# Relational layers of a four-layer graph network: dense columns in four chunks of 448, tables stored by half block and loaded whole

## The chip, the core and the metric

The kernel runs on one core of a Trainium2 chip. The metric is the time of one execution on the device in microseconds (us). The kernel before was timed three times: 2260.39 us in the median, 2258.17 to 2264.78. Its profile was taken from one more execution, which took 2260.0 us with a profiled span of 2258.2 us.

## What is computed

The input is a graph of N = 3125 nodes with 128 features, and 100,000 edges. Each edge has a source, a destination and one of 8 types; the edges are sorted by destination. Four layers follow one another, each with a residual sum and a layer norm. The change concerns the fourth alone, two relational convolutions:

```python
def rgcn_layer(x, src, dst, etype, W, W_root, b, num_rels):
    h = jnp.einsum('ni,rio->rno', x, W)
    msg = h[etype, src]
    seg = dst * num_rels + etype
    sums = jax.ops.segment_sum(msg, seg, num_segments=N * num_rels)
    cnt = jax.ops.segment_sum(jnp.ones(msg.shape[0], x.dtype), seg, num_segments=N * num_rels)
    mean = sums / jnp.maximum(cnt, 1.0)[:, None]
    agg = mean.reshape(N, num_rels, do).sum(axis=1)
    return agg + x @ W_root + b
...
h = jax.nn.relu(rgcn_layer(x, src, dst, edge_type, W1, root1, b1, 8))    # 128 -> 256
x = _layernorm(x + rgcn_layer(h, src, dst, edge_type, W2, root2, b2, 8)) # 256 -> 128
```

For each destination and each type, the features of its sources are averaged, and the averages go through that type's weights.

## The kernel before

**Stages.** Up to about 430 us the kernel builds, from the edge list, a matrix of edge counts between all nodes. From there to about 940 us the first three layers multiply by this matrix, five times. Beside these products a generator, `relations`, builds one table of counts for each type: `rel[r]` holds, for 14 of the 25 blocks of 128 destination nodes, how many edges of type r run from each of the 3200 (padded) sources. The entries are bytes; a block is stored as 128 rows (the source within its block) of 25 x 128 bytes (source block, destination). These 14 blocks are the dense columns. The other 11 blocks are the gathered ones: nothing is stored for them, and their edges are fetched one by one. At about 1014 us the two relational layers begin, layer 1 to about 1716 us, layer 2 to the end.

**Dense columns.** The 14 blocks are worked on in four chunks of 4, 3, 4 and 3 blocks, so 512, 384, 512 and 384 columns (the first four entries of `CH`, called `DENSE`). One call of `relation` takes one type and one chunk; it is called a pass here. There are 32 passes in each layer, numbered 0 to 63 over both. In layer 1 the chunk is the outer loop and the type the inner one, so passes 0 to 7 are chunk 0, passes 8 to 15 chunk 1, and so on. In layer 2 the type is outer and the chunk inner. A pass has five groups of five source blocks. For each group the sync queue (SP) loads a piece of the table into one of six buffers `m8` (L725); VectorE (DVE, L735, groups 0, 2 and 4) or ScalarE (ACT, L733, groups 1 and 3) casts the bytes to floats in one of three buffers `m`; and TensorE (PE, L738) runs ten matmuls, one with the high part and one with the low part of the features of each source block. VectorE then multiplies the pass's sum by the inverse counts, which the ACT queue has loaded (L853 in layer 1, L914 in layer 2, where L916 adds the result to the output).

**Gathered columns.** A second generator, `gathered`, handles these edges 128 at a time, 355 times in each layer: GpSimd (POOL, L772) fetches 128 rows of the features by an indirect DMA into one of twelve buffers `gx`, VectorE makes a one-hot matrix of destination and type (`oh`, L764), and three or six matmuls (L780) add the rows up. After each group of a pass the generator is moved on by 2.2 steps on average, beginning with a debt of 14 steps, so about 11 gathers belong to a pass and some 28 are left behind the last pass of a layer. When a chunk of gathered blocks is complete, its sums are scaled (`put1`, `put2`).

**Between the layers.** In layer 1, when all eight types of a chunk are done, `linear1` multiplies by the weights: transposes of the features (L812), 36 matmuls over the chunk's columns (L818, L820), relu (L821). Then, for each whole block, it makes the features that layer 2 needs for all 8 types (L828, eight matmuls a block) and stores them with `store3`, twice a block, into `ht_d` (L715, on the SP queue, from two buffers `t3`). `store3` also writes the input of layer 1, `xt_d`, in seven stores at the start of layer 1; every gather of layer 1 waits for all seven, every gather of layer 2 for all stores to `ht_d`. In layer 2, `fetch` reads one type's features back in five loads `back` (L865, also SP, two buffers), adds the pieces on VectorE (L868, L869) and splits them in two.

**Order.** Instructions of an engine run in the order of the built program; each waits for its operands. The order is set by a scheduler at build time, from the order in the source and its own estimates. The SP queue holds, in one order, the loads L725, the stores L715 and the loads L865: one that waits for a buffer holds up those behind it.

Of the kernel before, what the change touches and what calls it, by code (L numbers as in the profile page):

```python
# [21 lines left out]
P = 128  # L22
D = 128
N = 3125
NB = 25
NP = NB * P
R = 8
# [30 lines left out]
SL = 64  # L58
HL = 49 * 64
ND = 14  # L60
# [12 lines left out]
def listed(ctx: ExitStack, tc: tile.TileContext, p: dict, out: bass.AP, bad):  # L73


    nc = tc.nc
# [4 lines left out]
    ident = const.tile([P, P], F32, name="ident")  # L81
# [17 lines left out]
    dsf = dram.tile([E // 200, 200], F32, name="dsf")  # L99
    adj = dram.tile([NB, P, NP], BF, name="adj")  # L100
    adj_t = dram.tile([NB, P, NB, P], BF, name="adj_t")
    rel = [dram.tile([ND, P, NB, P], U8, name=f"rel{r}") for r in range(R)]
    inv_d = dram.tile([R * SB, 2 * P], F32, name="inv_d")

    inv_n = dram.tile([SB * 2 * P, R], F32, name="inv_n")
# [42 lines left out]
    with tc.tile_pool(name="f_bg", bufs=1) as bg, tc.tile_pool(  # L148
# [194 lines left out]
        def relations():  # L343
# [95 lines left out]
            for i, (b, u) in enumerate(units):  # L439
                lo, hq = nxt  # L440
                if i + 1 < len(units):
                    nxt = hots(*units[i + 1])
                if u == 0:
                    rb = bg.tile([P, R * NB, 64], U16, name="rb", bufs=2)
                for v in range(PU // 4):
                    pt = psum.tile([P, 4, 256], F32, name="bld", tag="bld", bufs=2)
                    for k in range(4):
                        j = v * 4 + k
                        nc.tensor.matmul(pt[:, k, : R * NB], lo[:, j // 2, :, j % 2], hq[:, j // 2, :, j % 2],  # L449
                                         start=True, stop=True)  # L450
                    j0 = u * PU + v * 4
                    o = rb[:, :, j0 : j0 + 4]
                    src = pt[:, :, : R * NB].rearrange("p j q -> p q j")
                    n += 1
                    if n % 5 < 4:
                        nc.scalar.copy(o, src)  # L456
                    else:
                        nc.vector.tensor_copy(o, src)  # L458
                    if v == 1:
                        yield  # L460
                if u == 64 // PU - 1:
                    for r in range(R):
# [214 lines left out]

    O1 = 256
    x3 = xa
    DENSE = [c for c in CH if c[0] < ND]  # L680
    with tc.tile_pool(name="f_rel", bufs=1) as rp, tc.tile_pool(
        name="f_psr", bufs=1, space=PSUM
    ) as psum:
# [2 lines left out]
        b1 = column("L3_gnn_b1", 2)  # L686
        b2 = column("L3_gnn_b2")

        def load_inv(r, m0, nb):
            t = rp.tile([P, 512], F32, name="inv", bufs=2)  # L690
            v = inv_d.rearrange("r c -> (r c)")[r * SB * 2 * P + m0 * P :]
            nc.scalar.dma_start(t[:, : nb * P], bcast(v, nb * P))
            return t[:, : nb * P]

        def pair():
            t = rp.tile([P, 2, NB, D], F32R, name="hilo", tag="big", bufs=2)
# [19 lines left out]

        ahead = [0.0]

        def relation(r, m0, nb, pieces, work, rate):

            acc = psum.tile([P, 512], F32, name="acc", tag="acc", bufs=2)
            w = nb * P
            for g in range(5):
                m8 = rp.tile([P, 4, 5, P], U8, name="m8", bufs=6)
                nc.sync.dma_start(  # L725
                    m8[:, :nb].rearrange("p b k d -> p b (k d)"),
                    rel[r][m0 : m0 + nb, :, 5 * g : 5 * g + 5].rearrange("b p k d -> p b (k d)"),
                )
                m = rp.tile([P, 5, 4 * P + 8], F32R, name="m", bufs=3)
                v = m[:, :, :w].rearrange("p k (b d) -> p k b d", d=P)  # L730
                src = m8[:, :nb].rearrange("p b k d -> p k b d")
                if g % 2:
                    nc.scalar.copy(v, src)  # L733
                else:
                    nc.vector.tensor_copy(v, src)  # L735
                for k in range(5):
                    for i, x in enumerate(pieces):
                        nc.tensor.matmul(  # L738
                            acc[:, :w], x[:, 5 * g + k, :],
                            m[:, k, :w],  # L740
                            start=(g == 0 and k == 0 and i == 0), stop=(g == 4 and k == 4 and i == 1),
                        )
# [4 lines left out]
            return acc[:, :w]  # L747

        def gathered(table, rows, put):

# [39 lines left out]
        with tc.tile_pool(name="f_z", bufs=1) as zp:  # L790
# [13 lines left out]
                store3(xt_d[m0 * P : (m0 + nb) * P].rearrange("(b p) c -> p b c", p=P),  # L804
                       x3[:, m0 : m0 + nb, :])

            def linear1(z, m0, nb):
                w = min(nb * P, HL - m0 * P)
                x3t = zp.tile([P, 512], F32, name="x3t", bufs=1)
                t = psum.tile([P, 512], F32, name="mi", tag="mi", bufs=2)  # L810
                for i in range(nb):
                    nc.tensor.transpose(t[:, cols(i, 1)], x3[:, m0 + i, :], ident)  # L812
                nc.scalar.copy(x3t[:, : nb * P], t[:, : nb * P])
                for a in range(2):
                    o = psum.tile([P, 512], F32, name="mi", tag="mi", bufs=2)
                    c = slice(a * P, (a + 1) * P)
                    for r in range(R):
                        nc.tensor.matmul(o[:, :w], w1[:, r, c], z[:, r, :w],  # L818
                                         start=(r == 0), stop=False)
                    nc.tensor.matmul(o[:, :w], root1[:, c], x3t[:, :w], start=False, stop=True)  # L820
                    nc.scalar.activation(hT[:, a, m0 * P : m0 * P + w], o[:, :w], AF.Relu,  # L821
                                         bias=b1[:, a : a + 1])

                for b in range(m0, m0 + nb):
                    for r in range(0, R, 4):
                        o = psum.tile([P, 512], F32, name="mi", tag="mi", bufs=2)
                        for a in range(2):
                            nc.tensor.matmul(o, hT[:, a, cols(b, 1)],  # L828
                                             wr[:, a, r : r + 4, :].rearrange("p r c -> p (r c)"),
                                             start=(a == 0), stop=(a == 1))  # L830
                        store3(ht_d.rearrange("(r n) c -> n r c", r=R)[b * P : (b + 1) * P, r : r + 4],
                               blocks(o))
# [3 lines left out]
            def put1(b, wn, acc, inv):  # L836
                m0, nb = [c for c in CH if c[0] <= b < c[0] + c[1]][0]
                if b == m0:
                    zg[0] = zp.tile([P, R, 512], F32, name="z", bufs=2)
                o = zg[0][:, :, (b - m0) * P : (b - m0) * P + wn].rearrange("p r n -> p n r")  # L840
                nc.vector.tensor_mul(o, acc.rearrange("p (n r) -> p n r", r=R),
                                     inv.rearrange("p (n r) -> p n r", r=R))
                if b == m0 + nb - 1:
                    linear1(zg[0], m0, nb)

            work = gathered(xt_d, gsrc[0], put1)
            ahead[0] = -14
            for m0, nb in DENSE:
                z = zp.tile([P, R, 512], F32, name="z", bufs=2)
                for r in range(R):  # L850
                    inv = load_inv(r, m0, nb)
                    acc = relation(r, m0, nb, xs, work, 2.2)
                    nc.vector.tensor_mul(z[:, r, : nb * P], acc, inv)  # L853
                linear1(z, m0, nb)
            for _ in work:
                pass

        with tc.tile_pool(name="f_hr", bufs=1) as hp:
# [47 lines left out]
            hr = fetch(0)  # L906
            for r in range(R):
                nxt = None
                for i, (m0, nb) in enumerate(DENSE):
                    inv = load_inv(r, m0, nb)  # L910
                    acc = relation(r, m0, nb, hr, work, 2.2)
                    s = hp.tile([P, 512], F32, name="s", bufs=2)
                    w = nb * P
                    nc.vector.tensor_mul(s[:, :w], acc, inv)  # L914
                    c = cols(m0, nb)
                    nc.vector.tensor_add(oT[:, c], oT[:, c], s[:, :w])  # L916
# [624 lines left out]
```

## Time and profile before

| what | time |
|---|---|
| three timed runs, median | 2260.39 us |
| the profiled execution | 2260.0 us |
| its span | 2258.2 us |
| TensorE busy in the span | 1955.4 us (87%) |
| VectorE busy | 1376.9 us (61%) |
| GpSimd busy | 954.5 us (42%) |
| first matmul of a dense pass | at 1014.6 us |
| first and last gather of layer 1 | at 1053.7 and 1662.4 us |
| first and last gather of layer 2 | at 1715.6 and 2242.2 us |

The profile gives the span in us from the first instruction. A row of a group has the line, the engine, the operation, the tile written and the tiles read, the shapes and the count; behind the first bar stand the group's busy time and the mean duration of one in ns, behind the second the engine's idle time before these instructions and what ended it. Digits are dropped from the names, so `m<-m` is the cast from `m8` to `m`, and `m<-rel` the load of `m8`. PEld is the load of TensorE's stationary operand. A row of a stretch has its bounds, its length, then busy time and count of PE, PEld, DVE, ACT and POOL, the granted clock of TensorE, the busy share of the 16 DMA engines and the GB/s they moved. A row of waits has who waited for whom: us in total, times, longest.

### The profile page before, as it was taken

What the parts mean: (1) busy time and instruction counts of PE and PEld (TensorE: products, weight loads), DVE (VectorE), ACT (ScalarE), POOL (GpSimd) and SP (SyncE); (2) the same over time, 40 slices, a digit from 0 to 9 for tenths busy, and PEclk for the clock granted to TensorE, in tenths of its full rate; (3) what the DMA queues carried; (4) which work ended last, traced back from release to release, by engine and by line L of the source; (5) the groups of instructions that cost most, each with busy time, mean ns of one, the idle gap of its engine ahead of it and who ended that gap; (6) DMA issues with size and microseconds to landing.
All of it is one profiled execution on the core that took longest, in us unless ns stands there. A gap on an engine that the chain in (4) does not pass through costs nothing. (4 is left out here: it accounts for less than half of the span.)

```text
span 2258.2 us, 32584 instructions
## 1 busy us (share of the span) xinstructions
PE 1955.4 (87%) x12551; PEld 1351.3 (60%) x12551; DVE 1376.9 (61%) x2385; ACT 791.5 (35%) x1027; POOL 954.5 (42%) x898
## 2 busy tenths in 40 slices
PE   1666669999999999957999999999878998899894
PEld 1444436666665555445668667758745776777772
DVE  4888889999996430045435345435337776666663
ACT  1666734545442110044223233233224333232230
POOL 3222121211210000002757547727723887777875
PEclk9777779999999999978999999999989999999996
DMA  3444476887888666427657467637637887788762
GB/s 93 176 189 166 178 193 211 287 284 257 272 277 269 180 193 177 120 60 222 173 140 212 139 185 213 187 117 207 172 99 219 241 238 221 201 229 228 199 172 77
DMA packets 384638, 433.10 MB, mean 192 GB/s; under 512 B 28731, under 2 KB 350301, under 8 KB 384472
## 3 DMA queue, kind: packets, MB, share of 16 engines
q1 hardware_dynamic: 314318, 278.95, 40.7%
q0 software_dynamic: 45920, 119.66, 18.2%
q10 hardware_dynamic: 24234, 32.31, 5.0%
q8 instruction: 100, 1.64, 0.3%
q14 instruction: 66, 0.54, 0.1%
HBM read 319.22 MB, written 111.58 MB: 191 GB/s over the span
## 5 line engine op out<-in xcount | busy, mean ns | idle before, releaser
L738 PE MATMUL acc<-m,hilo 128*128 128x384 f32 (+1 forms) x3200 | 758.5, 383 | 12.0 <-DVE m L735 6.6
L772 POOL DMA_INDIRECT gx<-xt_d,gsrc x355 | 393.6, 1109 | 573.2 <-DMA m<-rel 357.2
L738 PEld LDWEIGHTS acc<-m,hilo 128*128 128x128 f32 x3200 | 577.6, 193 | 80.3 <-issue 8.9
L539 PE MATMUL acc<-m,parts 128*128 128x512 bf16 (+1 forms) x2625 | 539.3, 357 | 15.7 <-issue 12.7
L772 POOL DMA_INDIRECT gx<-ht_d,gsrc x355 | 412.9, 1163 | 167.0 <-issue 56.4
L733 ACT CAST m<-m 128x1920 fp32r<-128x1920 uint8 (+1 forms) x128 | 264.2, 2064 | 540.1 <-PE acc L738 491.5
L735 DVE CAST m<-m 128x2560 fp32r<-128x2560 uint8 (+1 forms) x192 | 302.6, 1576 | 161.3 <-PE acc L738 92.5
L539 PEld LDWEIGHTS <-parts 128*128 128x128 bf16 x2625 | 255.3, 98 | 238.3 <-issue 17.9
L780 PE MATMUL ga<-oh,gx 128*128 128x192 bf16 (+1 forms) x2442 | 273.5, 246 | 98.8 <-DMA gx<-ht_d,gsrc 57.7
L780 PEld LDWEIGHTS <-gx 128*128 128x128 bf16 x2442 | 170.7, 99 | 206.9 <-DMA gx<-ht_d,gsrc 83.1
L456 ACT CAST rb<-bld 128x800 uint16<-128x800 f32 x179 | 143.9, 828 | 129.7 <-PE bld L449 121.4
L463 POOL DMA_DIRECT2D rel<-rb x112 | 64.3, 582 | 287.5 <-ACT rb L456 162.6
L764 DVE TENSOR_TENSOR oh<-iota,gkey 128x768 bf16<-128x768 bf16 (+1 forms) x188 | 99.5, 530 | 92.2 <-PE ga L780 89.2
L162 DVE TENSOR_TENSOR lo<-iota,kT 128x2048 bf16<-128x2048 bf16 x100 | 122.0, 1220 | 0.0
L712 DVE TENSOR_TENSOR e<-mi,t 128x512 f32<-128x512 f32 x50 | 34.3, 688 | 133.8 <-ACT t L711 133.8
L272 PE MATMUL bld<-hi,lo 128*128 128x50 bf16 x1600 | 74.4, 200 | 46.1 <-DVE hi L162 38.9
L449 PE MATMUL bld<-rhq,rlo 128*128 128x200 bf16 x896 | 107.6, 252 | 1.8 <-DVE rb L458 1.1
L272 PEld LDWEIGHTS <-lo 128*128 128x128 bf16 x1600 | 63.4, 107 | 70.6 <-DVE hi L162 26.3
L449 PEld LDWEIGHTS <-rlo 128*128 128x128 bf16 x896 | 82.4, 98 | 36.7 <-issue 9.0
L162 DVE TENSOR_TENSOR rhq<-iota,kT 128x3200 bf16<-128x3200 bf16 x56 | 102.2, 1824 | 0.0
L828 PE MATMUL mi<-wr,hT 128*128 128x512 f32 x200 | 93.9, 604 | 4.8 <-DVE e L712 4.7
L285 ACT ACTIVATE av<-mi 128x896 bf16<-128x896 bf16 (+1 forms) x100 | 82.8, 835 | 31.4 <-PE mi L284 30.1
(212 smaller groups left out, 1813.4 us busy)
## 6 DMA issues: line engine op xcount, KB each, us to landing
m<-rel SPq DMA_DIRECT2D x160, 320.0 KB, 4.1
rel<-rb POOLq DMA_DIRECT2D x112, 400.0 KB, 6.5
m<-adj SPq DMA_DIRECT2D x60, 640.0 KB, 7.3
m<-rel SPq DMA_DIRECT2D x160, 240.0 KB, 3.2
m<-adj_t SPq DMA_DIRECT2D x40, 640.0 KB, 4.1
m<-adj SPq DMA_DIRECT2D x45, 480.0 KB, 6.1
adj_t<-at SPq DMA_DIRECT2D x25, 800.0 KB
adj<-av SPq DMA_DIRECT2D x25, 800.0 KB, 3.3
```

Of the source, the lines that this page charges most:

```text
L162: nc.vector.tensor_tensor(o, (iota2 if of is None else of)[:, None, :width, :].to_broadcast([P, PU // 2, width, 2]), k[:, :, None, :].to_b ...
L272: nc.tensor.matmul(pt[:, j, : 2 * NB], lo[:, j // 2, :, j % 2], hi[:, j // 2, :, j % 2], start=True, stop=True)
L449: nc.tensor.matmul(pt[:, k, : R * NB], lo[:, j // 2, :, j % 2], hq[:, j // 2, :, j % 2], start=True, stop=True)
L456: nc.scalar.copy(o, src)
L539: nc.tensor.matmul(o, x[:, k, :], m(k - k0), start=(k == 0 and i == 0), stop=last and more is None)
L733: nc.scalar.copy(v, src)
L735: nc.vector.tensor_copy(v, src)
L738: nc.tensor.matmul(acc[:, :w], x[:, 5 * g + k, :], m[:, k, :w], start=(g == 0 and k == 0 and i == 0), stop=(g == 4 and k == 4 and i == 1),)
L764: nc.vector.tensor_tensor(oh[:, : nt // 2], iota2[:, None, : GW * R, :].to_broadcast([P, nt // 2, GW * R, 2]), gkey[:, g, t : t + nt].rear ...
L772: nc.gpsimd.indirect_dma_start(out=gx.rearrange("p i c -> p (i c)"), out_offset=None, in_=table[:], in_offset=bass.IndirectOffsetOnAxis(ap ...
L780: nc.tensor.matmul(acc[:, a:z], gx[:, i, :], oh[:, t % 4 // 2, a - c0 : z - c0, t % 2], start=(a // 512 not in seen), stop=(t == GT[g] - 1 ...
L828: nc.tensor.matmul(o, hT[:, a, cols(b, 1)], wr[:, a, r : r + 4, :].rearrange("p r c -> p (r c)"), start=(a == 0), stop=(a == 1))
```

## The change

The tables `rel[r]` are stored by half blocks of 64 destinations: 28 half blocks, each 128 rows of 25 x 64 bytes, 1600 bytes in one run where a row of a block was 3200. The staging tile `rb` in `relations` is ordered to match, and each of its 112 stores writes two half blocks.

The dense columns are cut into four chunks of 7 half blocks, 448 columns each. A pass loads its whole table, 1400 KB in 7 x 128 runs of 1600 bytes, with one DMA into one of two buffers `m8`, in place of five loads of 320 or 240 KB in runs of 640 bytes into six buffers. The casts have 5 x 7 x 64 elements, the matmuls 448 columns. `linear1` takes its first column and width, and the list of blocks that are whole by then: 3, 4, 3 and 4 of them where it was 4, 3, 4 and 3. A chunk that starts or ends in the middle of a block transposes that block too, so 16 transposes in the four dense chunks and not 14. `load_inv` loads 448 columns each time. The gathers are as before.

```diff
-    rel = [dram.tile([ND, P, NB, P], U8, name=f"rel{r}") for r in range(R)]
+    rel = [dram.tile([2 * ND, P, NB, 64], U8, name=f"rel{r}") for r in range(R)]
...
-                    rb = bg.tile([P, R * NB, 64], U16, name="rb", bufs=2)
+                    rb = bg.tile([P, 2, R * NB, 32], U16, name="rb", bufs=2)
...
-                    o = rb[:, :, j0 : j0 + 4]
+                    o = rb[:, j0 // 32, :, j0 % 32 : j0 % 32 + 4]
...
-                            rel[r][b].rearrange("p s d -> p (s d)").bitcast(U16),
-                            rb[:, r * NB : (r + 1) * NB, :].rearrange("p s j -> p (s j)"),
+                            rel[r][2 * b : 2 * b + 2].rearrange("h p s d -> p h (s d)").bitcast(U16),
+                            rb[:, :, r * NB : (r + 1) * NB, :].rearrange("p h s j -> p h (s j)"),
...
-    DENSE = [c for c in CH if c[0] < ND]
+    CW = 7 * 64
+    DENSE = [(7 * i, 7 * i // 2, (7 * i + 7) // 2 - 7 * i // 2) for i in range(2 * ND // 7)]
...
-        def relation(r, m0, nb, pieces, work, rate):
+        def relation(r, h0, pieces, work, rate):
             acc = psum.tile([P, 512], F32, name="acc", tag="acc", bufs=2)
-            w = nb * P
+            m8 = rp.tile([P, 7, NB, 64], U8, name="m8", bufs=2)
+            nc.sync.dma_start(m8.rearrange("p h k d -> p h (k d)"),
+                              rel[r][h0 : h0 + 7].rearrange("h p k d -> p h (k d)"))
             for g in range(5):
-                m8 = rp.tile([P, 4, 5, P], U8, name="m8", bufs=6)
-                nc.sync.dma_start(
-                    m8[:, :nb].rearrange("p b k d -> p b (k d)"),
-                    rel[r][m0 : m0 + nb, :, 5 * g : 5 * g + 5].rearrange("b p k d -> p b (k d)"),
-                )
-                m = rp.tile([P, 5, 4 * P + 8], F32R, name="m", bufs=3)
-                v = m[:, :, :w].rearrange("p k (b d) -> p k b d", d=P)
-                src = m8[:, :nb].rearrange("p b k d -> p k b d")
+                m = rp.tile([P, 5, CW + 8], F32R, name="m", bufs=3)
+                v = m[:, :, :CW].rearrange("p k (h d) -> p k h d", d=64)
+                src = m8[:, :, 5 * g : 5 * g + 5].rearrange("p h k d -> p k h d")
...
-            def linear1(z, m0, nb):
-                w = min(nb * P, HL - m0 * P)
+            def linear1(z, c0, w, whole):
+                b0 = c0 // P
...
-                for i in range(nb):
-                    nc.tensor.transpose(t[:, cols(i, 1)], x3[:, m0 + i, :], ident)
-                nc.scalar.copy(x3t[:, : nb * P], t[:, : nb * P])
+                for b in range(b0, -(-(c0 + w) // P)):
+                    nc.tensor.transpose(t[:, cols(b - b0, 1)], x3[:, b, :], ident)
+                nc.scalar.copy(x3t[:, :w], t[:, c0 - b0 * P : c0 - b0 * P + w])
...
-                for b in range(m0, m0 + nb):
+                for b in whole:
```

More of the change, by code (lines that the diff above doesn't have):

```diff
@@ L687, in listed, with load_inv @@
         b2 = column("L3_gnn_b2")
[L689 to L693, printed above, removed]
+        def load_inv(r, h0):
+            t = rp.tile([P, CW], F32, name="inv", bufs=2)
+            v = inv_d.rearrange("r c -> (r c)")[r * SB * 2 * P + h0 * 64 :]
+            nc.scalar.dma_start(t, bcast(v, CW))
+            return t
         def pair():
@@ L738, in relation @@
                         nc.tensor.matmul(
-                            acc[:, :w], x[:, 5 * g + k, :],
-                            m[:, k, :w],
+                            acc[:, :CW], x[:, 5 * g + k, :], m[:, k, :CW],
                             start=(g == 0 and k == 0 and i == 0), stop=(g == 4 and k == 4 and i == 1),
@@ L746, in relation @@
                     ahead[0] -= 1.0
-            return acc[:, :w]
+            return acc[:, :CW]
         def gathered(table, rows, put):
@@ L820, in linear1 @@
                     nc.tensor.matmul(o[:, :w], root1[:, c], x3t[:, :w], start=False, stop=True)
-                    nc.scalar.activation(hT[:, a, m0 * P : m0 * P + w], o[:, :w], AF.Relu,
+                    nc.scalar.activation(hT[:, a, c0 : c0 + w], o[:, :w], AF.Relu,
                                          bias=b1[:, a : a + 1])
-                for b in range(m0, m0 + nb):
+                for b in whole:
                     for r in range(0, R, 4):
@@ L843, in put1 @@
                 if b == m0 + nb - 1:
-                    linear1(zg[0], m0, nb)
+                    linear1(zg[0], m0 * P, min(nb * P, HL - m0 * P), range(m0, m0 + nb))
             work = gathered(xt_d, gsrc[0], put1)
             ahead[0] = -14
-            for m0, nb in DENSE:
+            for h0, m0, nb in DENSE:
                 z = zp.tile([P, R, 512], F32, name="z", bufs=2)
                 for r in range(R):
[L851 to L854, printed above, removed]
+                    inv = load_inv(r, h0)
+                    acc = relation(r, h0, xs, work, 2.2)
+                    nc.vector.tensor_mul(z[:, r, :CW], acc, inv)
+                linear1(z, h0 * 64, CW, range(m0, m0 + nb))
             for _ in work:
@@ L908, in listed @@
                 nxt = None
[L909 to L916, printed above, removed]
+                for i, (h0, m0, nb) in enumerate(DENSE):
+                    inv = load_inv(r, h0)
+                    acc = relation(r, h0, hr, work, 2.2)
+                    s = hp.tile([P, CW], F32, name="s", bufs=2)
+                    nc.vector.tensor_mul(s, acc, inv)
+                    c = slice(h0 * 64, h0 * 64 + CW)
+                    nc.vector.tensor_add(oT[:, c], oT[:, c], s)
                     if i == 0 and r + 1 < R:
```

## The prediction

> **What bounds the kernel now.** I read the groups of the page first, for what a pass costs, then stretches of single chunks, then GpSimd's waits, then the timeline where the gathers begin. The change touches the span from 1014 us on; before it, only the order in which the tables are stored. The groups:
>
> ```profile
> L738 PE MATMUL acc<-m,hilo 128*128 128x512 f32 x1600 | 424.8, 411 | 6.2 <-ACT m L733 3.6 <-ACT hilo L702 1.6 <-DVE m L735 0.8
> L738 PE MATMUL acc<-m,hilo 128*128 128x384 f32 x1600 | 333.7, 355 | 5.8 <-DVE m L735 5.8
> L735 DVE CAST m<-m 128x2560 fp32r<-128x2560 uint8 x96 | 170.6, 1778 | 83.7 <-PE acc L738 51.2 <-ACT m L733 16.5 <-issue 13.2
> L735 DVE CAST m<-m 128x1920 fp32r<-128x1920 uint8 x96 | 131.9, 1374 | 77.6 <-PE acc L738 41.3 <-issue 29.7 <-ACT m L733 6.6
> L818 PE MATMUL mi<-z,w 128*128 128x512 f32 x96 | 42.3, 593 | 0.6 <-DVE z L841 0.6
> L818 PE MATMUL mi<-z,w 128*128 128x384 f32 x96 | 32.0, 487 | 0.6 <-DVE z L841 0.6
> L828 PE MATMUL mi<-wr,hT 128*128 128x512 f32 x200 | 93.9, 604 | 4.8 <-DVE e L712 4.7
> ```
>
> Behind the bar stand busy time and the mean of one, which counts the overlap with its neighbours; busy time over count is the cost: 265.5 ns a matmul at 512 columns (424.8 / 1600), 208.6 at 384. Now the stretches: passes 2-7 (chunk 0), 9-13 (chunk 1), 17-22 (chunk 2), 25-30 (chunk 3), and layer 2 whole.
>
> ```profile
> 1044.60:1158.30 113.70, 98.75 (x546) 72.87 (x546) 49.95 (x48) 28.89 (x15) 82.04 (x75) 0.94 0.64 176
> 1200.00:1266.30 66.30, 60.62 (x441) 54.71 (x438) 32.73 (x37) 17.96 (x10) 52.02 (x47) 1.00 0.71 197
> 1358.50:1446.20 87.70, 87.70 (x526) 68.88 (x524) 47.29 (x44) 28.00 (x12) 69.81 (x59) 1.00 0.76 207
> 1528.00:1609.50 81.50, 73.27 (x518) 64.90 (x515) 42.01 (x48) 23.17 (x15) 64.43 (x57) 1.00 0.71 196
> 1716.00:2243.00 527.00, 462.82 (x2834) 376.04 (x2832) 347.37 (x467) 158.14 (x109) 412.33 (x355) 0.94 0.75 208
> ```
>
> TensorE is idle for 14.95, 5.68, 0 and 8.23 us in layer 1's four chunks (length less the first busy time) and for 64.2 us in layer 2. What paces it there is GpSimd; first its waits in layer 1, then in layer 2, then its tile in layer 2:
>
> ```profile
> POOL gx L772 <- PE ga L780: 132.5, 80, 22.2
> ```
>
> ```profile
> POOL gx L772 <- PE ga L780: 31.2, 80, 6.6
> ```
>
> ```profile
> L772 POOL DMA_INDIRECT gx<-ht_d,gsrc x355: 940/948/2772, 1715.6 to 2242.2; - x178
> ```
>
> In layer 1 GpSimd stands still for 132.5 us with its twelve buffers full, mostly while TensorE works on `linear1`. In layer 2 it waits 31.2 us in 80 pieces, of which one is 6.6. It issues 355 gathers in 526.6 us, 1.48 us each, beginning to end. Layer 2 is set by the gathers, layer 1 by TensorE with gaps where gathers come late. The beginning of the gathers:
>
> ```profile
> 1044.92 3.72 SPq L725 DMA_DIRECT2D m<-rel  x2
> 1048.88 0.36 SPq L715 DMA_DIRECT2D xt_d<-t  x1
> ...
> 1053.71 1.05 POOL L772 DMA_INDIRECT gx<-xt_d,gsrc  x1 [357.22 <-DMA m<-rel]
> ```
>
> The seventh `xt_d` store is issued at 1048.88 behind loads of `m8` and lands just ahead of 1053.71, when GpSimd starts. The `m<-rel` named as its releaser is only what came last by the profile.
>
> **Costs that cancel.** A 448-column matmul is taken half way: (265.5 + 208.6) / 2 = 237 ns, so 3200 of them cost 758.5 us as before. The DVE cast is (1778 + 1374) / 2 = 1576 ns, 192 x 1.576 = 302.6 us, unchanged; ACT's (2331 and 1796, so 2064) likewise. That a cast out of 64-byte pieces keeps its rate no row shows. The two rows give 0.63 ns an element and 0.16 us besides; nothing speaks for less, and were it two thirds more (1.05 ns, so 2.5 us), DVE would be busy 347 + 96 x 0.93 = 436 of 527 us in layer 2, still not the bound. I take no change. The 112 table stores keep their bytes in twice as many runs; between 430 and 940 us TensorE is busy 507.8 of 510 us and POOL, which issues them, 50.1. That idle time hides them; without it they would cost 0.58 us each, 65 us.
>
> **Costs that move.** In the timeline of single records matmuls start 233 ns apart at 512 columns and 176 at 384, so 204.5 at 448: 28.5 ns x 50 = 1.4 us less for each pass of chunks 0 and 2, and 1.4 more in chunks 1 and 3. In `linear1`, 36 matmuls are 0.441 us at 512 and 0.333 at 384, so 1.9 us either way; a whole block at L828 is 8 x 0.47 = 3.8 us. With 3, 4, 3, 4 whole blocks: -5.8 us for chunks 0 and 2, +5.8 for 1 and 3. The two extra transposes are within a microsecond.
>
> **The load.** One DMA of 1400 KB replaces five. Rows: 320 KB in 4.1 us, 240 in 3.2, a slope that gives 16 us at 1400 KB; 640 KB of `adj_t` in runs of 1280 bytes 4.1, 480 KB 3.6, a slope that gives 6.5.
>
> ```profile
> m<-rel SPq DMA_DIRECT2D x160, 320.0 KB, 4.1
> m<-adj_t SPq DMA_DIRECT2D x40, 640.0 KB, 4.1
> m<-rel SPq DMA_DIRECT2D x160, 240.0 KB, 3.2
> m<-adj_t SPq DMA_DIRECT2D x30, 480.0 KB, 3.6
> ```
>
> I take 6.5 (its runs of 1280 bytes are nearest to 1600). With two buffers the load for pass r+2 is issued when the last cast of pass r is done, about 2/5 into TensorE's work on r, and needed a cast ahead of r+2: 1.6 passes less a cast, 1.6 x 13.1 - 2 = 19 us in layer 1, 23 in layer 2 at 15.5 a pass. Both prices fit, so I cost the wait at 0. The cover in layer 2 is 64.2/32 = 2 us of idle TensorE per pass; later than that, each microsecond counts.
>
> Behind that load on SP wait the `xt_d` and `ht_d` stores and the `back` loads. By the order of the built programs, the last `xt_d` store used to have its data written on DVE behind a cast of pass 2 and now behind the first cast of pass 3, for which TensorE must have come to matmul 130 in place of 100, and it stands behind the whole load for pass 4. The later data is 30 x 204.5 ns = +6.1 us; the narrower 100 matmuls give back 2.9; the first whole load costs +1 (0 to 4) at the start; the load ahead costs 0 to 3.5. Together +4, bounds 0 to +13.
>
> The Trainium skill, "DMA: Bandwidth & Descriptors", section on queues, rings and completion order, says that an engine's descriptors are consumed in ring order. By it that store's bytes wait for all 1.4 MB ahead, which at its derated 368 GB/s is an estimate of 3.9 us, and my sum would be +6 and not +2; no run here has yet shown so long a load.
>
> **Sum, as the shift of each landmark of layer 1.** Chunk 0 is paced by gathers, so its narrower passes gain nothing and its end shifts by the later start: +4. `linear1` -5.8: -1.8. Pass 8 +1.4; passes 9-13 +7.1, of which 5.7 fills idle time; passes 14-15 +2.8: +3.8, and 1 us of gaps there fills too: +2.8. `linear1` +5.8: +8.6. Chunk 2 would gain 8 x 1.4 = 11.3, but its 13.1-us passes receive 13.1 / 1.42 = 9.2 gathers where 10.7 are due (1.42 us is GpSimd's pace in layer 1), and twelve full buffers cover only that many; I take -8, bounds -11.3 to -4.5: +0.6. `linear1` -5.8: -5.2. Chunk 3 +11.3 less its 8.2 idle: -2.1. The last `linear1` +5.8: +3.7; but in pass 31 TensorE stood 10.4 us for gathers (its timeline), which can take up what came before; I let it take 3.7 (bounds 0 to 10.4), so layer 1 ends at 0. The `ht_d` stores held behind a whole load delay the first gather of layer 2 by a third of its 6.5 us: +2 (bounds 0 to 6.5). In layer 2 the gathers set the pace and are not changed: 0 (bounds -8, with the 6.6-us wait gone and a little more, to +8, were each gather 1.5% slower in the bursts of the loads). Sum: 2260.0 + 2 = **2262 us**; the profiled execution is 0.4 below the median, so both bases give this.
>
> **Rivals.** (1) *Faster: balance pays.* The start shifts by 1 and not 4, chunk 2 gains its full 11.3, and of pass 31's waits another 5 are filled: 2262 - 3 - 3.3 - 5 = 2250. For it: 13.9 us of idle time in the two narrow chunks. Against: it is the gathers that are late there, and equal passes don't bring more of them. (2) *Slower: a late start.* The gathers begin at the upper bound, +13, and each stretch stays gather-paced: 2262 + 9 + 4 = 2275. For it: the 357 us in which GpSimd waits for that one chain. Against: the 132.5 us in which it later waits for buffers. (3) *Slower: whole loads are late.* In layer 2 a load stands on SP behind `back` loads, which in the timeline wait up to 14 us for their two buffers; with the 16-us price that makes 30 against a window of 23, so 7 us late twice at each of seven fetches, less 8 us of cover in a type's four passes: 7 x (14 - 8) = 42, 2304. It decides once delay and load together exceed 23 + 2 us. For it: five pieces spread over six buffers need no such window. Against: at 6.5 us, 20.5 fits. (4) The change doesn't do what it says, each long load breaking up into short transfers: then it costs 16 us, without a delay inside the window, and the time is 2262 again, so it has no chance of its own.
>
> **How the numbers follow.** A measurement of this kernel tells about 0.3%, 6.8 us, from no change. Forecast (2253 to 2267, no change) 0.38; rival 1 0.29; rival 2 0.20; rival 3 0.13. Faster 0.29, same 0.38, slower 0.33. Below 2246 lies a fifth of rival 1 (0.06), above 2284 rival 3 and a little of rival 2 (0.14), so the range is 2246 to 2284.
>
> **What would show it.** The first gather of layer 1 at about 1058; TensorE's idle time below 6 us in chunk 3 but some 3 in chunk 2; dense matmuls busy 758 us; DVE's cast at 1576 ns; the load landing in some 6.5 us with no idle time of casts put down to it; 355 gathers of layer 2 in 527 us. The forecast is wrong if layer 2 grows by more than 8 us (then a load or the gathers' bursts set it), or if the gathers of layer 1 start later than 1067.

## The result, and the profile after

The changed kernel takes 2270.39 us in the median of seven runs (2264.66 to 2275.25), the kernel before 2260.39; the ratio is 1.0046, with an interval of 1.0034 to 1.0057. It is slower, by 0.5%. The profiled execution took 2268.9 us with a span of 2267.1, 8.9 us more than before. First the groups of the page that answer to those of before:

```profile
L738 PE MATMUL acc<-m,hilo 128*128 128x448 f32 x3200 | 770.2, 387 | 9.4 <-DVE m L735 4.7
L771 POOL DMA_INDIRECT gx<-xt_d,gsrc x355 | 395.7, 1115 | 578.7 <-DMA inv<-inv_d 359.4
L771 POOL DMA_INDIRECT gx<-ht_d,gsrc x355 | 417.3, 1175 | 164.0 <-issue 62.7
L735 DVE CAST m<-m 128x2240 fp32r<-128x2240 uint8 x192 | 301.7, 1572 | 131.8 <-PE acc L738 121.2
```

The cast costs what the two old shapes give half way (1572 ns, 1576 forecast), so pieces of 64 bytes are no burden to it. The dense matmuls are busy 11.7 us longer than the 758.5 forecast. The whole load, in the page's list of DMA issues:

```profile
m<-rel SPq DMA_DIRECT2D x64, 1400.0 KB, 7.5
```

The 7.5 us are the median of the 6 loads, of 64, whose landing the trace gives.

The stretches of the changed kernel, with the same passes as before: 2-7, 9-13, 17-22, 25-30, and layer 2 (columns as before: bounds, length, then PE, PEld, DVE, ACT and POOL, granted clock, DMA share, GB/s). Each begins with the first dense matmul of its first pass; the first ends with pass 7.

```profile
1041.60:1160.40 118.80, 95.95 (x540) 76.23 (x539) 44.77 (x46) 24.96 (x15) 81.38 (x76) 0.87 0.53 162
1198.40:1271.60 73.20, 68.64 (x441) 58.61 (x439) 34.74 (x37) 20.64 (x10) 57.97 (x51) 0.98 0.64 201
1370.90:1456.50 85.60, 80.07 (x525) 68.69 (x523) 44.52 (x46) 25.98 (x14) 67.83 (x58) 1.00 0.65 204
1531.30:1616.90 85.60, 81.18 (x518) 69.85 (x515) 46.85 (x49) 26.88 (x16) 67.79 (x59) 0.98 0.67 209
1723.50:2252.40 528.90, 465.40 (x2835) 389.44 (x2833) 347.40 (x466) 158.76 (x109) 416.79 (x355) 0.93 0.67 207
```

The first stretch, passes 2 to 7, is longer: TensorE is idle for 22.85 us of it (14.95 before), and its length is 118.8 us against 112.5 from the first dense matmul of pass 2 to the end of the last of pass 7 before. Chunk 2, whose passes had no idle TensorE at 512 columns, now has 5.5 us of it (85.6 less 80.1), and passes 17 to 22 are only 2.1 us shorter. Layer 2 is as long as before (528.9 against 527.0). The DMA engines are busy 0.64 to 0.67 of the time in the last four, for about the GB/s that took 0.71 to 0.76: long runs cost them less. Nothing was waiting for that.

Where the 10 us are is seen best by four distances from the clearing of `hT` (a MEMSET that marks the end of the layers before) to the last gather of layer 1. They are differences of start times in the traces; two profiles of each kernel, and two kernels of the experiments, are set beside each other:

| kernel | `hT` to first dense matmul | to the issue of the seventh `xt_d` store | to the first gather | first to last gather | sum |
|---|---|---|---|---|---|
| before | 10.6 | 34.2 | 4.8 | 608.7 | 658.3 |
| before, again | 10.4 | 34.3 | 4.6 | 608.6 | 657.9 |
| 448 columns, loads in pieces | 9.4 | 37.7 | 3.8 | 607.7 | 658.6 |
| changed | 14.2 | 34.3 | 6.0 | 614.0 | 668.5 |
| changed, again | 13.9 | 34.4 | 6.1 | 614.2 | 668.7 |
| old columns, whole loads | 14.7 | 36.5 | 6.2 | 612.4 | 669.8 |

In this table all kernels with whole loads have the 10 us, and none of the others has. From there on (the way to layer 2, and layer 2) they differ by some 3 us (595.8 to 599.0), without order.

### The profile page after: what moved, and what is told of

It is laid out like the page before. It is cut to its first block, busy times and chain, and to the rows that moved or that the text cites. A ratio compares the mean times of both kernels' runs of the same rounds, so it can differ in the third digit from the quotient of the medians.

```text
span 2267.1 us, 32002 instructions
## 1 busy us (share of the span) xinstructions
PE 1958.9 (86%) x12521; PEld 1377.5 (61%) x12553; DVE 1375.8 (61%) x2385; ACT 792.7 (35%) x1027; POOL 980.9 (43%) x898
## 4 chain that ended last, share of the span: by engine, by line
PE 55%; DMA 20%; DVE 13%; issue 6%; ACT 3%; POOL 3%; ACTq 0%; DVEq 0%; POOLq 0%
PE acc L738 19%; PE acc L540 17%; DMA gx<-ht_d,gsrc 8%; DMA gx<-xt_d,gsrc 6%; PE ga L779 5%; PE mi L818 4%; PE mi L828 3%; PE bld L450 2%; DVE lo L163 2%; DMA g<-dsf,irow 2%; POOL gx L771 2%; DVE hi L163 2%; DVE rhq L163 1%; PE mi L556 1%; DMA back<-ht_d 1%
## 5 line engine op out<-in xcount | busy, mean ns | idle before, releaser
L738 PE MATMUL acc<-m,hilo 128*128 128x448 f32 x3200 | 770.2, 387 | 9.4 <-DVE m L735 4.7
L771 POOL DMA_INDIRECT gx<-xt_d,gsrc x355 | 395.7, 1115 | 578.7 <-DMA inv<-inv_d 359.4
L738 PEld LDWEIGHTS acc<-m,hilo 128*128 128x128 f32 x3200 | 601.7, 196 | 60.2 <-issue 10.3
L540 PE MATMUL acc<-m,parts 128*128 128x512 bf16 (+1 forms) x2593 | 533.3, 357 | 17.6 <-issue 12.7
L771 POOL DMA_INDIRECT gx<-ht_d,gsrc x355 | 417.3, 1175 | 164.0 <-issue 62.7
L733 ACT CAST m<-m 128x2240 fp32r<-128x2240 uint8 x128 | 264.2, 2064 | 565.3 <-PE acc L738 495.9
L735 DVE CAST m<-m 128x2240 fp32r<-128x2240 uint8 x192 | 301.7, 1572 | 131.8 <-PE acc L738 121.2
L464 POOL DMA_DIRECT2D rel<-rb x112 | 84.9, 761 | 268.3 <-ACT rb L457 152.8
L715 DVE TENSOR_TENSOR e<-mi,t 128x512 f32<-128x512 f32 x50 | 34.3, 687 | 134.8 <-ACT t L714 131.2
```

What stands on the lines that cost most here:

```text
L540: nc.tensor.matmul(o, x[:, k, :], m(k - k0), start=(k == 0 and i == 0), stop=last and more is None)
L738: nc.tensor.matmul(acc[:, :CW], x[:, 5 * g + k, :], m[:, k, :CW], start=(g == 0 and k == 0 and i == 0), stop=(g == 4 and k == 4 and i == 1),)
L771: nc.gpsimd.indirect_dma_start(out=gx.rearrange("p i c -> p (i c)"), out_offset=None, in_=table[:], in_offset=bass.IndirectOffsetOnAxis(ap ...
```

## The experiments

Twelve runs were made, of ten kernels. Theory W, the first one formed after the result, put the cost on the equal widths; rival L on the whole loads.

**First four, on a chip that decided little.** The old columns with one whole load a pass (the small tile `x3t` shares the buffers of `e3`, for room):

```diff
+            m8 = rp.tile([P, 4, NB, P], U8, name="m8", bufs=2)
+            nc.sync.dma_start(m8[:, :nb].rearrange("p b k d -> p b (k d)"),
+                              rel[r][m0 : m0 + nb].rearrange("b p k d -> p b (k d)"))
             for g in range(5):
-                m8 = rp.tile([P, 4, 5, P], U8, name="m8", bufs=6)
-                nc.sync.dma_start(
-                    m8[:, :nb].rearrange("p b k d -> p b (k d)"),
-                    rel[r][m0 : m0 + nb, :, 5 * g : 5 * g + 5].rearrange("b p k d -> p b (k d)"),
-                )
...
-                src = m8[:, :nb].rearrange("p b k d -> p k b d")
+                src = m8[:, :nb, 5 * g : 5 * g + 5].rearrange("p b k d -> p k b d")
...
-                x3t = zp.tile([P, 512], F32, name="x3t", bufs=1)
+                x3t = rp.tile([P, 512], F32, name="x3t", tag="e3", bufs=2)
```

> The old chunks of 512, 384, 512 and 384 columns and the old table of whole blocks, but each pass loads its table with one DMA (1600 or 1200 KB) into one of two buffers. Theory W (widths): the 10 us come from the equal widths alone, because passes of layer 1 are paced by the gathers for much of the time, so that narrower passes in chunks 0 and 2 gain little and wider ones in chunks 1 and 3 cost. Then this kernel stays within 4 us of the kernel before, 2257 to 2264. Rival L (loads): the whole loads cost it, by holding up the stores behind them on SP and by slowing the gathers in bursts. Then 2267 to 2273, and the first gather of layer 1 some 2 to 4 us later than 1053.7.

The new columns with five loads:

```diff
-            m8 = rp.tile([P, 7, NB, 64], U8, name="m8", bufs=2)
-            nc.sync.dma_start(m8.rearrange("p h k d -> p h (k d)"),
-                              rel[r][h0 : h0 + 7].rearrange("h p k d -> p h (k d)"))
             for g in range(5):
+                m8 = rp.tile([P, 7, 5, 64], U8, name="m8", bufs=6)
+                nc.sync.dma_start(m8.rearrange("p h k d -> p h (k d)"),
+                                  rel[r][h0 : h0 + 7, :, 5 * g : 5 * g + 5].rearrange("h p k d -> p h (k d)"))
...
-                src = m8[:, :, 5 * g : 5 * g + 5].rearrange("p h k d -> p k h d")
+                src = m8.rearrange("p h k d -> p k h d")
```

> Four chunks of 448 columns and the table by half blocks, but the table loaded in five pieces into six buffers as before, in runs of 320 bytes. Theory W: 2267 to 2273, as the changed kernel, with the dense matmuls idle in the same places. Rival L: 2257 to 2264. If the short runs make a load take longer than about 8 us, casts would wait for it and both figures rise.

The changed kernel with the `xt_d` stores on another queue:

```diff
-        def store3(rows, x):
+        def store3(rows, x, q=None):
...
-            nc.sync.dma_start(rows, t[:, :n].rearrange("p b i c -> p b (i c)"))
+            (q or nc.sync).dma_start(rows, t[:, :n].rearrange("p b i c -> p b (i c)"))
...
-                       x3[:, m0 : m0 + nb, :])
+                       x3[:, m0 : m0 + nb, :], nc.scalar)
```

> The changed kernel with the seven stores of xt_d issued from the ACT queue in place of SP, so that no whole load stands ahead of them. Theory W: the first gather of layer 1 starts 0 to 2 us earlier than at 1056.2 and the time falls by as much, 2268 to 2271. Rival L: the start moves to 1050 or so and the time to 2262 to 2265.

And the old chunks in another order:

```diff
-    DENSE = [c for c in CH if c[0] < ND]
+    DENSE = [(0, 3), (3, 4), (7, 3), (10, 4)]
```

> The kernel before with its dense chunks in the order 384, 512, 384, 512, loads as before. The same columns, so TensorE has the same work. Theory W: the move is twice that of the change (128 columns a chunk and not 64): chunk 0 is narrow and paced by gathers (gains nothing), chunk 1 wide (8 x 2.8 = 22 us, less 6 of idle time), chunk 2 narrow (gains 5 at most), chunk 3 wide (22 less 8 to 18 of idle time): 2272 to 2282. Rival L, and any theory by which only TensorE's work counts: 2257 to 2264.

These ran on a chip on which the kernel before took 2314.34 us. The ratios to it were 0.9999 (interval 0.9979 to 1.002), 0.9994 (0.9973 to 1.0016), 0.9959 (0.9934 to 0.9983) and 1.0007 (0.9987 to 1.0027). The changed kernel itself was not among them, so the third says only that this variant is 0.4% faster than the kernel before there, not what the stores' place is worth. The fourth speaks against W, as a move of columns twice that of the change cost nothing where W had 12 us or more; but the first shows nothing of the whole loads there either, so on this chip neither theory could be decided. What was different on that chip is a kind of idle time that no profile of the other chips has. The waits of TensorE in layer 1 of the kernel with the swapped order:

```profile
PE ga L780 <- issue: 29.2, 37, 3.0
...
PE acc L738 <- issue: 7.4, 17, 1.3
```

"issue" is time in which the engine waited for nothing that the profile shows: 36.6 us in these two rows, 29 to 32 us in the other three kernels on this chip, none in those of the kernel before and of the changed one elsewhere. Against such a background 10 us may be hidden; that it was is not shown. So the two decisive kernels were run again.

**Controls and two causes of waiting, on a chip where the kernel before takes 2258.63 us.** First the two kernels as they are:

> The changed kernel itself, beside the kernel before, on the chip of these runs. The three kernels that carry one part of the change, or twice one part, came out at ratios of 1.000, 0.999 and 1.001 to the kernel before on a chip where that takes 2314 us and not 2260. Theory J (jointly): the two parts cost only together, and the ratio is 1.003 to 1.006 here too. Rival C (chip): the change costs nothing of its own on such a chip, where gathers pace layer 1 more than on the first one, and the ratio is 0.998 to 1.002.

> The kernel before, for a profile of it on the chip of these runs. If gathers take longer here, as rival C has it, TensorE's idle time in layer 1 put down to gathers is 10 us or more above the 53 us of the first profile.

The ratio was 1.0065 (1.0046 to 1.0084), 2272.92 us; theory J holds, in that the cost is there again, and nothing on how it is made up is shown by it. Rival C falls. The second profile of the kernel before is in the table above; TensorE's waits for gathers in its layer 1 are no longer than in the first (37.3 us against 37.8).

Then the casts, four of five on ACT:

```diff
-                if g % 2:
+                if g != 2:
```

> The changed kernel with four of the five casts of a pass on ACT and one on DVE (before: two and three). If layer 2 is set by GpSimd, whose gathers take 0.94 us alone and 1.35 us beside a DVE cast, the mean gather of layer 2 falls from 1.175 us to about 1.04 and layer 2 from 544 to 500 us, layer 1 by 5 to 15: 45 to 60 us less than the changed kernel. If a wait of TensorE for casts or the load decides instead, the time stays or rises, as ACT needs 2.06 us a cast and DVE 1.57.

2201.6 us, ratio 0.9753 (0.9731 to 0.9776): 71 less than the changed kernel on the same chip, more than the 45 to 60 expected. Its groups:

```profile
L733 ACT CAST m<-m 128x2240 fp32r<-128x2240 uint8 x256 | 527.0, 2064 | 311.3 <-PE acc L738 272.1
L771 POOL DMA_INDIRECT gx<-xt_d,gsrc x355 | 361.5, 1018 | 582.0 <-ACT m L733 356.1
L735 DVE CAST m<-m 128x2240 fp32r<-128x2240 uint8 x64 | 100.7, 1574 | 0.0
```

The mean gather of layer 1 falls from 1115 to 1018 ns, that of layer 2 from 1175 to 1074, and layer 2 (from its first dense matmul to the end) from 544 to 507 us. In the changed kernel a gather takes 945 ns in the mean while VectorE is idle, and 1366 (layer 1) or 1388 (layer 2) beside one of its casts; 292 of the 710 gathers stood beside a cast, and 103 after the edit. So DVE's casts had been holding up GpSimd.

Then gathers inside the dense `linear1`:

```diff
-            def linear1(z, c0, w, whole):
+            def linear1(z, c0, w, whole, work=iter(())):
...
                     for r in range(0, R, 4):
+                        for _ in range(3):
+                            next(work, None)
...
-                    acc = relation(r, h0, xs, work, 2.2)
+                    acc = relation(r, h0, xs, work, 1.9)
...
-                linear1(z, h0 * 64, CW, range(m0, m0 + nb))
+                linear1(z, h0 * 64, CW, range(m0, m0 + nb), work)
```

> The changed kernel with gathers put between the matmuls of the dense chunks' linear1 too, six to a block, and fewer in the passes (rate 1.9 for 2.2 in layer 1). If layer 1 is paced by gathers in its passes while GpSimd stands still with full buffers in linear1 (115 us in the trace of the changed kernel), GpSimd's standing falls by 30 to 60 us, TensorE's idle time in layer 1 by 15 to 30, and the time by 10 to 25. If TensorE's work alone sets layer 1, the time stays within 4 us.

2230.97 us, ratio 0.9884 (0.9864 to 0.9904): 42 less than the changed kernel where 10 to 25 were expected. GpSimd's waits with full buffers in layer 1, the changed kernel first and then this one:

```profile
POOL gx L771 <- PE ga L779: 137.4, 85, 20.2
```

```profile
POOL gx L771 <- PE ga L779: 93.7, 88, 15.8
```

They fall by 44 us, and layer 1 by 35 (708 to 673 us, first dense matmul to first dense matmul). So layer 1 is paced by gathers in its passes, and GpSimd's standing still during `linear1` costs time.

**The two decisive kernels again, on a chip where the kernel before takes 2260.66 us.**

> Once more the old chunks and the old table with one whole load a pass, now beside kernels that settle the same question; on a chip where the kernel before takes about 2259 us. Theory W (widths): within 4 us of the kernel before, and passes 17 to 23 take 87 to 89 us with TensorE idle under 2 us in them. Rival L (loads): 8 to 14 us more than before.

> Once more four chunks of 448 columns with five piecewise loads into six buffers, on a chip where the kernel before takes about 2259 us. Theory W: 8 to 14 us more than before; from the start of pass 0 to that of pass 16 8 us more than the 326 us of before, chunk 2 no shorter. Rival L: within 4 us of the kernel before.

The old columns with whole loads took 2270.39 us, ratio 1.0045 (1.0029 to 1.0062). The new columns with loads in pieces took 2258.28, ratio 0.9989 (0.9977 to 1.0002). Theory W falls and rival L holds: the whole load alone costs what the change cost (ratios of 1.0046 and 1.0065), and the equal widths alone cost nothing. Of W's details in the second little came true: from pass 0 to pass 16 that kernel takes 3.4 us longer than before (329.4 against 326.0, the mean of two profiles) and not 8, and its passes 17 to 22 are 4.9 us shorter (82.8 against 87.7).

**Both edits, with either set of columns and loads.**

> The changed kernel with both earlier edits: four casts of five on ACT, and gathers between the matmuls of the dense linear1 at rate 1.9 in layer 1. Layer 2 should take the 507 us of the run with the casts, 37 less than the changed kernel; layer 1 fills the same idle time by both edits, 42 to 55 us less and not the sum of 33 and 35: 2165 to 2195. If the two gains don't overlap, 2160 or less.

> The same two edits in the kernel before (512, 384, 512 and 384 columns, piecewise loads). Theory W: with gathers no longer setting the pace of layer 1's passes, widths don't matter, and it is within 6 us of the run above. Rival L, or any other standing cost of the change: 8 to 15 us less than the run above.

The changed kernel with both edits takes 2180.95 us (ratio 0.9652, 0.9636 to 0.9668) and the kernel before with both 2188.16 (0.9684, 0.9668 to 0.9699). Both are 3% faster than either kernel of the change, and the first is the fastest of all. Here the whole loads show no cost in the total: TensorE waits 9.4 us for gathers in layer 1 with them and 14.0 with pieces, against 43.5 in the changed kernel, and from first to last gather of layer 1 it is 556 and 557 us. The late start is still there (19.8 us from `hT` to the first dense matmul, 16.6 with pieces). Neither theory had the kernel with whole loads ahead by 7; that difference was not followed up, and as these two kernels differ in widths as well as in loads, it doesn't tell what either is worth. New columns with pieces and both edits were not tried.

## Why the prediction was right in size and wrong in cause

The time lay within 2246 to 2284, but beyond the forecast's own range (2253 to 2267), and 0.5% is not "no change"; rival 2's 2275 was nearer than the forecast's 2262. By its steps:

**The load "fits, so I cost the wait at 0".** This is the step that failed. Its price was nearly right, 7.5 us against 6.5 taken, and that both fit the window was right as well: in the changed kernel one cast, the first, waited for a whole load, and none of the other 319. But I asked only who waits for the load. The runs show that whole loads cost 10 us all the same, and the traces show the loss in three places, beside the load and not in a wait for it.

First, the start of the stage. I had the first whole load at +1 (0 to 4), for the first cast. In the table the first dense matmul is 3.6 us later (14.2 against 10.6). Here is ACT in the changed kernel, in its timeline, engine and its queue (ACTq) together:

```profile
1004.61 0.46 ACT L135 ACTIVATE xa<-bld,ng,rs 128x128 f32<-128x128 f32 x1 [0.44 <-DVE ng L131]
1004.62 5.74 ACTq L794 DMA_DIRECT2D wr<-in_L_gnn_W  x1
1010.40 0.46 ACT L135 ACTIVATE xa<-bld,ng,rs 128x128 f32<-128x128 f32 x1 [5.33 <-issue]
1010.42 4.65 ACTq L796 DMA_DIRECT2D root<-in_L_gnn_root  x1
1015.12 0.62 ACT L705 CAST hilo<-xa 128x512 fp32r<-128x512 f32 x1 [4.26 <-issue]
```

And in the kernel before:

```profile
1010.44 0.37 ACTq L795 DMA_DIRECT2D wr<-in_L_gnn_W  x1
1011.37 0.46 ACT L134 ACTIVATE xa<-bld,ng,rs 128x128 f32<-128x128 f32 x1 [0.48 <-DVE xa L137]
1011.37 2.50 ACTq L797 DMA_DIRECT2D root<-in_L_gnn_root  x1
1013.91 0.62 ACT L702 CAST hilo<-xa 128x512 fp32r<-128x512 f32 x1 [2.08 <-issue]
```

Two whole loads, 2800 KB, had been issued on SP at 1001.71 and 1002.12. While they are under way, ACT's two issues of the weights `wr` and `root1` take 5.74 and 4.65 us, where before they took 0.37 and 2.50, and ACT does nothing else meanwhile. The split of the features into `hilo` stands behind them, and the first dense matmul behind the split. The old columns with whole loads show the same (7.50 and 3.44), the new columns with pieces don't (0.38 and 1.97). No later issue on ACT in layer 1 of the changed kernel took over 0.5 us.

The 0.37 is no fair mark, though: in the kernel before, ACT came to that issue 6.4 us after the clearing of `hT` and not 2.95, because VectorE's first cast stood ahead of a step of the normalisation. Counted from `hT`, the split begins after 9.9 and 9.7 us before, 8.7 with the new columns and pieces, 13.5 and 13.2 in the changed kernel, and 14.0 with the old columns and whole loads. The kernel before with both edits, which has pieces and comes to that issue after 4.0 us, needs 9.9, so the order of the instructions is not the reason.

What ACT stands for are its own weights: 2048 KB of `w1` and `wr` are ahead of `root1` on its queue. In ten profiles from chips where the kernel before takes about 2260 us, the issue of `root1` ends when 1.34 to 1.41 MB have moved on that queue. How fast they move is read from the DMA packets between 1011 and 1014 us:

| kernel | run of the table, bytes | SP's queue: packets, MB | ACT's queue: packets, MB |
|---|---|---|---|
| 448 columns, loads in pieces | 320 | 1051, 0.33 | 1046, 0.53 |
| before | 640 | 722, 0.44 | 719, 0.52 |
| changed | 1600 | 441, 0.71 | 442, 0.41 |
| old columns, whole loads | 3200 | 274, 0.88 | 279, 0.29 |

The two queues move equally many packets, a packet of the table is one run, and so the weights get less the longer the runs are. A whole load has longer runs than the pieces and also puts more at once on SP's queue; no run separates the two.

Second, the last `xt_d` store. SP and GpSimd in the changed kernel:

```profile
1047.52 0.36 SPq L726 DMA_DIRECT2D m<-rel  x1
1050.14 0.36 SPq L718 DMA_DIRECT2D xt_d<-t  x1
1056.18 1.93 POOL L771 DMA_INDIRECT gx<-xt_d,gsrc  x1 [359.36 <-DMA inv<-inv_d]
```

The store is issued 2.6 us after the load for pass 4. The load's packets run to 1053.3, the store's first begins at 1052.9, 2.7 us after its issue, and the last ends at 1054.4; the gathers start 1.8 us later. Before, with pieces of 320 KB ahead, the store's first packet came 1.8 us after its issue, and with the new columns in pieces, with no load just ahead, 0.9. From store to gather it is 6.0 us where it was 4.8: a price of 1.2, within the 0 to 3.5 given, of which the +4 took nothing. With the stores on ACT's queue it was 5.0 (one profile, on the chip of the first four). The rule of consumption in ring order from the Trainium skill, "DMA: Bandwidth & Descriptors", section on queues, rings and completion order, names this order, and these times agree with it; the estimate of 3.9 us was too many, because the load had run 2.6 us when the store was issued.

The other part of that step, +6.1 for later data less 2.9 for narrower matmuls, came to nothing: from first dense matmul to the store it is 34.2 us before and 34.3 after. The narrower matmuls and the table that is already there (the kernel before waits 0.8 and 2.8 us for casts in passes 0 and 1, the changed one 1.0 and nothing) about made up for the matmuls that came in addition (143 had started when that store was issued, 119 before). The first gather was forecast 4 us later, at about 1058; it came at 1056.18, 2.5 later, and 4.9 later when counted from `hT` (the kernels reach that point 2 us apart). The +4 was a right sum of wrong terms, so luck.

Third, and largest, 5.4 us between the first gather and the last of layer 1. They are lost in passes 2 to 7: these take 118.8 to 118.9 us in the three profiles with whole loads, and 112.3 to 113.5 in the three without. TensorE's waits for gathers in layer 1, in the kernel before, the new columns with pieces, the changed kernel, and the old columns with whole loads:

```profile
PE ga L780 <- DMA gx<-xt_d,gsrc: 37.8, 40, 3.6
```

```profile
PE ga L779 <- DMA gx<-xt_d,gsrc: 36.4, 37, 3.2
```

```profile
PE ga L779 <- DMA gx<-xt_d,gsrc: 43.5, 39, 4.3
```

```profile
PE ga L778 <- DMA gx<-xt_d,gsrc: 40.5, 34, 3.5
```

In the mean a wait is longer: 43.5 / 39 = 1.12 us against 37.8 / 40 = 0.95. Measured on the gathers that TensorE waited for more than 0.25 us, from their issue to their first matmul, it is 3.95 us in the mean before and 4.65 in the changed kernel, 4.04 with the new columns and pieces, 4.82 with the old columns and whole loads; the slowest tenth are above 5.3, 6.5, 5.2 and 6.5. So with whole loads these gathers come later. In the changed kernel this can account for the loss: in passes 2 to 7 its waits for gathers are 22.6 us, 14.3 before. With the old columns and whole loads it can't: there they are 13.1 us, and TensorE is busy 104.4 us in place of 98, at a granted clock of 0.87 where it was 0.94. The new columns with pieces have 0.86 there and lose 1 us at most, so the clock alone is not the reason either. Why passes 2 to 7 take 6 us longer in both kernels with whole loads stays open.

That whole loads are the cause is shown by the two runs; how the 10 us divide over these three places is read from the traces (3.6, 1.2, 5.4), and no run has taken one place away by itself beside the changed kernel. To load only the first table in pieces, or to issue the weights earlier, would do that; neither was tried.

**Chunk 2's -8 (bounds -11.3 to -4.5).** In the changed kernel passes 17 to 22, six of the eight, gained 2.1 us, and nothing in its second profile (87.7 us, as before); with pieces they gained 4.9 (82.8). From pass 16 to pass 25, so with chunk 2's `linear1` and pass 24, the forecast's terms make 12.4 us less (8 and 5.8, less 1.4); the traces show 6.6 and 4.7 less, and 7.6 with pieces. So the forecast was right that something caps the gain in chunk 2, and wrong in its size. A reason would be that twelve buffers are not twelve gathers in hand, since those that have not yet landed are among them; that is not shown. Together with the load's 10 us this makes most of the difference between the forecast's landmarks and the trace: pass 16 forecast +8.6, measured +9.9; pass 25 forecast -3.8 (the -5.2 behind `linear1` and 1.4 for pass 24), measured +3.3; the first gather of layer 2 forecast +2, measured +7.4. At pass 16 the agreement is luck: with pieces it is +1.8, so most of the shift there is the load's and not that of the widths.

**Costs that cancel.** Right for the casts. The table stores take longer now (84.9 us busy on POOL), but the clearing of `hT`, which comes after them, is at 1001.7 to 1004.1 us in all six profiles of the table, without order. The dense matmuls' 11.7 us more are not the width alone: with the new columns and pieces they are busy 761.5 us.

**Layer 2 at 0.** Right: 528.4 us from first to last gather, 526.6 before. TensorE's waits for gathers grew there too (60.0 us, 46.9 before), and cost nothing where GpSimd sets the pace.

**The rivals.** Rival 2 named the right place, the late start, but priced it at 13 us and tied it to the order of the stores; 4.9 came, most of it by a queue that it did not look at. Rival 1 did not come: the equal columns without whole loads ran at 0.9989. Rival 3 did not: its loads were not late. The doubt in the fourth, that the load would cost 16 us, is settled by the 7.5.

## What to carry to other kernels

A transfer that is in time for its own consumer is not free: ask what is issued while it is under way, on every queue, and whether anyone stands waiting for those transfers (here weights, stores and gathers). Large loads at the start of a stage may belong behind the smaller ones that open it, which was not tried here; and of two queues at work the one with the longer runs took the larger share of the bytes. Where gathers set the pace, look first for what keeps their engine from running ahead; giving it work during `linear1` and taking casts off VectorE were worth 42 and 71 us here, each alone, where the layout moved 10.

## What the runs showed of the hardware that had not been expected

- Issuing a DMA from ACT took up to 7.75 us (5.74 in the changed kernel), in place of 0.4, while its own earlier weights and two whole loads were under way, and the engine's own instructions stood still meanwhile.
- Two DMA queues that were both at work moved packets one for one (441 and 442 in 3 us in the changed kernel, 1051 and 1046 with pieces), so their shares of the bytes went by the length of their runs, from 320 to 3200 bytes.
- Table loads in runs of 320 bytes did no harm: the new columns with pieces ran at a ratio of 0.9989, with a DMA share of 0.79 to 0.80 in the last four stretches where runs of 1600 bytes gave 0.64 to 0.67.
- On one chip the kernel before took 2314 us and not 2260, and in the four kernels profiled there TensorE had 29 to 37 us of idle time in layer 1 that nothing in the profile ends. The old columns with whole loads, at a ratio of 1.0045 on another chip, measured 0.9999 on it.
